# A scan layer in chunks of 64 tokens with two heads stacked, centred weights in front of seven norms, and attention sums first on TensorE

## The chip, the cores and the metric

The kernel runs on one core of a Trainium2 chip. A core has TensorE (PE in the profile, its weight loads PEld), VectorE (DVE), ScalarE (ACT), GpSimd (POOL), a queue that issues most transfers (SP), 128-partition on-chip memory, and eight accumulator banks of 128 x 512 fp32 that TensorE writes. The metric is the device time of one execution in microseconds; lower is better.

## The reference

4096 tokens of width 128 pass through eight residual layers. Each layer is followed by a layer norm without weights, all in fp32:

```python
x = layernorm(x + counter_mix(x))        # layer 0: concat[x, softplus(count)] @ W2
x = layernorm(x + ffn_binarised(x))      # layer 1: gelu(x @ bw1.T + b1) @ bw2.T + b2
x = layernorm(x + channel_attention(x))  # layer 2: per token and head a causal 64 x 64 softmax, then @ Wo + bo
x = layernorm(x + ffn_ternary(x))        # layer 3
x = layernorm(x + gated_linear_attn(x))  # layer 4: o @ Wo
x = layernorm(x + four_experts(x))       # layer 5: relu(x @ W1 + b1) @ W2 + b2, weighted
x = layernorm(x + mamba2(x))             # layer 6: 16 heads of 8 channels, state 64, then @ W_out
x = layernorm(x + kronecker_moe(x))      # layer 7
```

Layer 6 is a linear recurrence over 512 tokens. `dt = softplus(x @ W_dt + b)`, `A = -exp(A_log) * dt`, `B = x @ W_B`, `C = x @ W_C`. With the tokens cut into chunks, a chunk's output is `(C B^T * exp(decay)) X` from inside the chunk (the part `within`) plus `C @ state` from the chunks before (the part `across`), and the state is carried on by `state = state * exp(sum A) + B^T (decayed X)`. The result does not depend on the chunk length; the reference itself uses 64.

## The kernel before

**Tiles and groups.** The tokens are 32 tiles of 128. Eight blocks of four tiles go through layers 0 and 1 (`front`); nine groups (seven of four tiles, two of two, `SIZES`) go through layers 3 to 7.

**Layer 2.** The channel attention is the bulk. Each tile is two units of 64 tokens; each unit is 17 pieces (64 units, 1088 pieces). A piece is a product query x key on DVE (two of 17 on POOL), a subtraction of the row maximum on POOL, an exponential on ACT, a sum over keys on TensorE (`den`), a product with the value on DVE, and a second sum on TensorE (`num`). The pieces live in a ring buffer of `ERING` columns (tile `ringe`); `feed` puts pieces in, `rest` carries each through, `close` finishes a tile and does its norm.

**Order of the work.** No engine order is written by hand. All layers are Python generators that yield the engine they need next. `Order.run` builds one fixed order per engine: it holds an estimated clock for each engine and takes the task that can start first; among tasks within `EPS` = 0.05 us on the same engine the smallest rank wins (`URGE`: close 0, prepare 1, chains 2, rest 3, feed 4). `urge` gives rank 9 to a chain that is ahead of its pace (`LAG`). There are three chains: `chain_a` (fronts and layers 3 to 5), `chain_b` (layer 6), `chain_c` (layer 7). They run beside the attention of later groups; after the last attention piece they are alone. All helpers record their instructions through one line, so nearly every row of the profile says L60, and tiles are told apart by name.

**Matmuls.** `Tensor.matmul` (line 67) splits a product with 128 rows of contraction into column pieces of 32, four of which stand on the array at a time. An fp32 matmul gives two records in the trace.

**A norm** (`norm`, line 545, after layers 0, 1, 3, 4, 5, 6). DVE adds the residual into the accumulator bank, takes `bn_stats` and `bn_aggr` of each tile (`stats`, line 530); ACT makes the reciprocal deviation and the shift (`shifts`) and applies both; TensorE transposes. In layer 5 the residual comes in with the last expert. `close` (line 982) has the same for one tile, with the last step on DVE.

**Layer 6** (line 1309) works on chunks of one tile by four heads: `chunk(j, hq)`, 16 for a group of four tiles. A chunk projects B and C (16 column pieces on TensorE into one bank, one copy by ACT to tile `bc`); ACT multiplies the mask `U` with A for each head (`em`, 128 x 128); TensorE turns that into log decays (`mask16` and `SL` times `em`), ACT takes the exponential. `within` multiplies B and C of each head on TensorE (64 rows, 128 columns, two banks `pg`), DVE multiplies the two halves with `em`, and TensorE adds the product with X (`xp`) to the sums of two tiles. `across` adds `state` x C, transposes B, multiplies it with `dx`, and DVE updates the state with two `scalar_tensor_tensor` (128 x 8 each). `drain` gates the sums; a last matmul with `Wout` and `norm` end the layer.

Of the kernel before, what the change touches and what calls it, by code (L numbers as in the profile page):

```python
# [31 lines left out]
ERING = 8904  # L32
# [6 lines left out]
    "f2_bu": 1, "a3_bdt": 16, "a3_Alog": 16, "f3_sup": 1, "f3_sdn": 1, "bup": 64, "bdn": 32, "rep": 32, "SL": P, "U": P,  # L39
# [98 lines left out]
class Order:  # L138
# [100 lines left out]
    def urge(self, t):  # L239

        if t.rank in self.pace:
            group, steps, size = self.pace[t.rank]
            lag, total = LAG[t.rank]
            if group + size * min(1.0, steps / total) > self.place - (lag if group < HURRY else 0.0):
                return 9
        return self.rank[t.rank]
# [73 lines left out]
class Model:  # L320
# [4 lines left out]
    def __init__(self, ctx, tc, a):  # L325
# [13 lines left out]
            "x": (5, 512), "xT": (5, 512), "a": (6, 512), "b": (12, 512), "c": (4, 512), "gt": (1, 1024), "xp": (2, 152),  # L339
# [76 lines left out]
    def start(self):  # L416
# [23 lines left out]
        for i in range(3):  # L440
            self.d.dma_start(left[32 * i : 32 * i + 2], a["bias"])
        for i in range(3):
            self.v.tensor_copy(part, left[:66])
            self.v.tensor_copy(self.bias[32 * i : 32 * i + 2], part[32 * i : 32 * i + 2])
            self.v.tensor_tensor(left[:66], left[:66], part, ALU.subtract)
# [4 lines left out]
        self.d.dma_start(self.Wo, a["a1_Wo"].rearrange("(c p) d -> p c d", p=P))  # L450

# [7 lines left out]
        self.state = self.keep([P, 8, 32], "state")  # L459
# [3 lines left out]
        self.negA = self.keep([P, H], "negA")  # L463
# [5 lines left out]
        self.mask16 = self.keep([P, P], "mask16", dtype=BF16)  # L469
        self.v.tensor_scalar(self.mask16, self.k["SL"], -30000.0, None, ALU.mult)  # L470
# [73 lines left out]

    def norm(self, g, c, r):

        x = g.x
        mv, rs = yield from self.stats(r, c)
        nm = self.shifts(c, mv, rs)
        for j in range(g.n):  # L550
            self.s.activation(x[:, j, :], r[:, j, :], AF.Identity, scale=rs[:, j : j + 1], bias=nm[:, j : j + 1])
        self.drop(r)
        yield from self.transpose(g.xT, [x[:, j, :] for j in range(g.n)])
# [50 lines left out]
    def count(self, g, nT):  # L604
# [18 lines left out]
        w = yield from self.load("a", self.a["a0_W2"].rearrange("(c p) d -> p c d", p=P), 2, D)  # L623
# [6 lines left out]
        yield "DVE"  # L630
        self.v.tensor_tensor(po, g.x, po, ALU.add)
# [23 lines left out]
    def binarise(self):  # L655

        for half, n, count in ((0, 1, D), (1, 4, 512)):
# [22 lines left out]
            self.v.tensor_tensor(wT, wT, bw, ALU.add)  # L680
            self.drop(ab, bw, alpha)
# [4 lines left out]
            self.drop(wT)  # L686

# [17 lines left out]
    def layer1(self, g):  # L705
# [15 lines left out]
        for j in range(TPG):  # L721
# [3 lines left out]
            for f in range(4):  # L725
                self.pe.matmul(
                    po[:, j, :], lhsT=hT[:, f, j * P : (j + 1) * P], rhs=w2T[:, f * D : (f + 1) * D],
                    start=False, stop=(f == 3),
                )
        yield "DVE"  # L730
        self.v.tensor_tensor(po, g.x, po, ALU.add)
# [250 lines left out]
    def close(self, unit):  # L982
# [22 lines left out]
        if u == 1:  # L1005
# [10 lines left out]
            st, mv, rs = self.small([P, 6], "cst"), self.small([P, 2], "cmv"), self.small([P, 1], "crs")  # L1016
            self.v.tensor_tensor(po, x, po, ALU.add)
            self.v.bn_stats(st, po)
            self.v.bn_aggr(mv, st)
            yield "ACT"  # L1020
            self.rstd(rs, mv[:, 1:2])
            yield "DVE"
            self.v.tensor_scalar(x, po, mv[:, 0:1], rs, ALU.subtract, ALU.mult)
# [10 lines left out]
    def ternarise(self):  # L1034
        self.w3 = []
        for half in range(2):
# [18 lines left out]
            self.v.scalar_tensor_tensor(wT, wT, hi, neg, ALU.is_gt, ALU.subtract)  # L1055
            self.drop(pg, neg)
# [5 lines left out]
    def layer3(self, g):  # L1062
# [37 lines left out]
        for j in range(n):  # L1100
            yield "PE"
            for f in range(4):
                self.pe.matmul(
                    po[:, j, :], lhsT=hT[f][:, j * P : (j + 1) * P], rhs=prT[:, f * D : (f + 1) * D],
                    start=(f == 0), stop=(f == 3),
                )
        yield "DVE"
        self.v.tensor_tensor(po, g.x, po, ALU.add)
# [5 lines left out]
    def layer4(self, g):  # L1114
# [89 lines left out]
        Wo = yield from self.load("a", a["a2_Wo"], D)  # L1204
# [12 lines left out]
        for j in range(n):  # L1217
            self.pe.matmul(po[:, j, :], lhsT=og[:, j * P : (j + 1) * P], rhs=Wo, start=True, stop=True)
        yield "DVE"
        self.v.tensor_tensor(po, g.x, po, ALU.add)  # L1220
# [4 lines left out]
    def layer5(self, g):  # L1225
# [4 lines left out]
        def fetch(e):  # L1230
# [3 lines left out]
            self.d.dma_start(ew[e][1], a["f2_W2"][512 * e : 512 * e + 512].rearrange("(c p) d -> p c d", p=P))  # L1234
# [74 lines left out]
    def layer6(self, g):  # L1309
        a, xT, n = self.a, g.xT, g.n  # L1310
        SL, U = self.k["SL"], self.k["U"]
        yield "SP", self.free("b", 2)
        w, room = self.new("b"), self.new("b")
        X = room[:, : n * D].rearrange("p (j h q) -> p j h q", h=H, q=8)
        wbcs = {}

        def weights():
            for hq in range(4):
                yield "SP", self.free("b", 1 if n == TPG else 6)
                wbcs[hq] = self.new("b")  # L1320
                for i, name in enumerate(("WB", "WC")):
                    self.d.dma_start(wbcs[hq][:, 256 * i : 256 * i + 256], a["a3_" + name][:, 256 * hq : 256 * hq + 256])
# [3 lines left out]
        self.d.dma_start(Wout, a["a3_Wout"])  # L1326
        Xf = X.rearrange("p j h q -> p j (h q)")

        little = room[:, n * D : n * D + 40 * n] if n < TPG else self.small([P, 40 * n], "little", bufs=1)
        dt, A = (little[:, 16 * n * i : 16 * n * (i + 1)].rearrange("p (j h) -> p j h", h=H) for i in range(2))  # L1330
        over = little[:, 32 * n :].rearrange("p (j e) -> p j e", e=8)
# [5 lines left out]
        def inner(j):  # L1337
            yield "PE", self.free("bg")
            ps = self.new("bg")
            self.pe.matmul(ps[:, :144], lhsT=xT[:, j * P : (j + 1) * P], rhs=Wx, start=True, stop=True)  # L1340
            yield "ACT"
            self.s.copy(Xf[:, j, :], ps[:, :D])
            yield "DVE"
            self.v.tensor_tensor(dt[:, j, :], ps[:, D : D + H], self.k["a3_bdt"], ALU.add)
            self.drop(ps)

        yield from self.together(*(inner(j) for j in range(n)))
        yield "ACT", self.free("bg")
        ps = self.new("bg")[:, : 2 * n * H].rearrange("p (i j h) -> p i j h", i=2, h=H)
# [3 lines left out]
        self.v.tensor_tensor(A, dt, self.negA[:, None, :].to_broadcast([P, n, H]), ALU.mult)  # L1353
        yield "DVE"
        self.v.tensor_tensor(X, X, dt[:, :, :, None].to_broadcast([P, n, H, 8]), ALU.mult)
# [4 lines left out]
        pa = ps[:, : 2 * n * H].rearrange("p (i j h) -> p i j h", i=2, h=H)  # L1360
        for i, m in enumerate((SL, self.ones)):
# [5 lines left out]
        for e in range(2):  # L1367
            rows = slice(64 * e, 64 * e + 64)
            self.s.activation(over[rows], pa[rows, 1].rearrange("p j (t e) -> p j t e", e=2)[:, :, :, e], AF.Exp)
        if n == TPG:  # L1370
            dx = self.small([P, n, H, 8], "dx", bufs=1)
            yield "DVE"
        else:
            yield "DVE", self.free("b", 4)
            dx = self.new("b", n, H, 8)
        self.v.tensor_tensor(dx, X, pa[:, 0, :, :, None].to_broadcast([P, n, H, 8]), ALU.mult)
# [18 lines left out]
        def add(t, jj, what, i, lhsT, rhs):  # L1395
            sums, done = bank(t)
            done[i] += 1
            self.pe.matmul(
                sums[32 * i : 32 * i + 32, jj, what, :], lhsT=lhsT, rhs=rhs, start=done[i] == 1, stop=done[i] == 16
            )  # L1400

        def chunk(j, hq):
            cols, at, hs = slice(j * P, (j + 1) * P), 4 * j + hq, slice(4 * hq, 4 * hq + 4)

            yield "PE", self.free(
                "bg", also=lambda: count["begun"] == at and hq in wbcs and min(moved) >= j - 1,
                at=lambda: self.order.until(wbcs[hq]), b=3,
            )
            count["begun"] += 1
            bc, em, ps = self.new("b", 4, P), self.new("b", 4, P), self.new("bg", 4, P)  # L1410
            wbc = wbcs[hq].rearrange("p (i c) -> p i c", c=P)
            for i in range(4):
# [640 lines left out]
```

## Time and profile before

| | us |
|---|---|
| median of three runs (lowest, highest) | 3926.63 (3926.17, 3935.69) |
| the profiled execution, its own time | 3931.12 |
| its span, first to last instruction | 3929.3 |
| busy: PE, PEld | 3079.9, 1610.6 |
| busy: DVE, ACT, POOL | 3258.2, 2605.7, 2920.9 |
| mean granted TensorE clock | 0.909 |

"Busy" of an engine is the time that at least one of its instructions ran. A row of a group view gives count, busy time, mean length in ns, then the idle time of the engine ahead of it and what ended that. A row of the windows view gives the window, its length, and each engine's busy time in it with the number of records. A timeline row gives start, length and the number of instructions merged into it. The trace's first attention product on DVE starts at 88 us, and the last attention sum on TensorE at 3537 us.

### The profile page before, as it was taken

How to read it: one execution, taken by the hardware profiler on the slowest of the kernel's cores; microseconds unless marked ns; L12 is line 12 of the kernel's file. 1: busy time of each engine (PE TensorE's matmuls, PEld its weight loads, DVE VectorE, ACT ScalarE, POOL GpSimd, SP SyncE). 2: the span in 40 equal slices, each digit the busy share in tenths (PEclk: the TensorE clock that was granted, in tenths of full speed). 3: DMA queues.
4: the chain of work that ended last, by engine and by line, in shares of the span. 5: the costliest groups of instructions: out<-in, count | busy, mean ns of one | idle time of the engine just before them, and what ended most of it. 6: DMA issues, size and time to landing. Idle time of an engine off the chain costs nothing.

```text
span 3929.3 us, 128714 instructions
## 1 busy us (share of the span) xinstructions
PE 3079.9 (78%) x55472; PEld 1610.6 (41%) x55472; DVE 3258.2 (83%) x4477; ACT 2605.7 (66%) x4970; POOL 2920.9 (74%) x1320
## 2 busy tenths in 40 slices
PE   6676676777788887977888977888888887879873
PEld 2232222433344443543444543544444443446652
DVE  3779889898998899899898889999989989983421
ACT  5576565667667885677657875787657786666530
POOL 1879997899788887788878877889778987870010
PEclk8798788888899998999999999999989999999986
DMA  3221122212223334243423323343423334424465
GB/s 89 57 53 44 44 59 59 62 44 52 50 59 90 85 79 104 67 117 76 111 61 96 98 74 87 86 126 78 106 64 94 96 88 104 103 63 141 140 154 111
DMA packets 385297, 331.30 MB, mean 84 GB/s; under 512 B 196108, under 2 KB 320460, under 8 KB 384728
## 3 DMA queue, kind: packets, MB, share of 16 engines
q1 hardware_dynamic: 375384, 289.53, 29.8%
q0 software_dynamic: 9344, 33.56, 2.8%
q8 instruction: 434, 7.11, 0.7%
q14 instruction: 135, 1.11, 0.1%
HBM read 147.85 MB, written 40.89 MB: 48 GB/s over the span
## 4 chain that ended last, share of the span: by engine, by line
PE 29%; DVE 27%; ACT 17%; POOL 13%; issue 9%; DMA 4%; SPq 1%; DVEq 0%; POOLq 0%; ACTq 0%
DVE ringe L60 18%; PE bg L60 16%; POOL ringe L60 13%; ACT ringe L60 8%; PE den L60 6%; PE num L60 5%; DVE bg L60 4%; PE kvr L60 3%; ACT ha L60 2%; ACT b L60 1%; ACT L60 1%; ACT bg L60 1%; SPq L60 1%; DVE a L60 1%; DVE b L60 1%
## 5 line engine op out<-in xcount | busy, mean ns | idle before, releaser
L60 POOL TENSOR_TENSOR ringe<-ringe,mr 128x1024 f32<-128x1024 f32 (+13 forms) x1088 | 2557.7, 2386 | 476.1 <-DVE ringe L60 313.3
L60 DVE TENSOR_TENSOR ringe<-ringe,kvr 128x1024 f32<-128x1024 f32 (+14 forms) x1093 | 1287.6, 1208 | 165.3 <-PE den L60 131.5
L60 ACT ACTIVATE ringe<-ringe 128x1664 f32<-128x1664 f32 (+14 forms) x964 | 997.7, 1055 | 600.0 <-POOL ringe L60 597.7
L60 DVE TENSOR_TENSOR ringe<-qr,kvr 128x1024 f32<-128x1024 f32 (+12 forms) x960 | 1103.0, 1184 | 34.7 <-PE num L60 21.1
L60 PE MATMUL den<-ringe,cst 128*32 128x128 f32 (+7 forms) x8744 | 701.8, 416 | 250.5 <-ACT ringe L60 209.4
L60 PE MATMUL num<-ringe,cst 128*32 128x256 f32 (+7 forms) x8720 | 702.5, 410 | 237.6 <-DVE ringe L60 229.8
L60 PEld LDWEIGHTS den<-ringe,cst 128*32 128x32 f32 x8744 | 235.9, 114 | 563.7 <-ACT ringe L60 349.4
L60 PEld LDWEIGHTS num<-ringe,cst 128*32 128x32 f32 x8720 | 227.4, 113 | 566.5 <-DVE ringe L60 440.0
L60 ACT ACTIVATE ringe<-ringe,cst 128x256 f32<-128x256 f32 x512 | 356.7, 780 | 52.1 <-POOL ringe L60 51.9
L60 POOL TENSOR_TENSOR ringe<-qr,ks 128x896 f32<-128x896 f32 (+1 forms) x128 | 287.1, 2243 | 56.0 <-PE num L60 30.0
L60 PE MATMUL bg<-xT,a 128*32 128x512 f32 (+1 forms) x1912 | 253.5, 623 | 34.1 <-DVE a L60 10.0
L60 DVE TENSOR_TENSOR_SCAN bg<-ends,bg 128x512 f32<-128x512 bf16 x128 | 155.0, 1217 | 23.1 <-PE bg L60 22.9
L60 PE MATMUL kvr<-wkv,xT 128*32 128x256 f32 x2048 | 152.0, 419 | 25.9 <-DVE ringe L60 25.6
L60 PE MATMUL bg<-a,ha 128*32 128x128 f32 x4800 | 163.9, 279 | 8.8 <-ACT ha L60 8.5
L60 ACT COPY b<-bg 128x256 f32<-128x256 f32 (+2 forms) x226 | 100.3, 451 | 80.1 <-PE bg L60 75.6
L60 PEld LDWEIGHTS bg<-a,ha 128*32 128x32 f32 x4800 | 132.1, 113 | 30.3 <-issue 14.8
L60 PE MATMUL bg<-xT,b 128*32 128x128 f32 (+1 forms) x3456 | 126.9, 289 | 9.7 <-DVE b L60 3.8
L60 ACT ACTIVATE b<-cst,little 128x128 f32<-128x128 f32 x420 | 133.7, 397 | 0.0
L60 ACT ACTIVATE ha<-bg,cst 128x512 f32<-128x512 f32 (+1 forms) x155 | 100.9, 670 | 38.5 <-PE bg L60 38.1
L60 PE MATMUL bg<-b,cst 128*32 128x512 f32 x856 | 118.9, 627 | 7.9 <-ACT b L60 7.9
L60 PEld LDWEIGHTS bg<-xT,b 128*32 128x32 f32 x3456 | 102.1, 116 | 43.4 <-issue 15.2
L60 PEld LDWEIGHTS bg<-xT,a 128*32 128x32 f32 x1912 | 60.8, 117 | 130.7 <-issue 59.2
(679 smaller groups left out, 4391.5 us busy)
## 6 DMA issues: line engine op xcount, KB each, us to landing
qr<-q SPq DMA_DIRECT2D x512, 128.0 KB
mr<-t SPq DMA_DIRECT2D x512, 128.0 KB
a<-in_f_W SPq DMA_DIRECT2D x67, 256.0 KB
c<-tu SPq DMA_DIRECT2D x204, 64.0 KB
tu<-gt SPq DMA_DIRECT2D x24, 512.0 KB
td<-gt SPq DMA_DIRECT2D x24, 512.0 KB
c<-in_f_Wdn SPq DMA_DIRECT2D x47, 256.0 KB
c<-td SPq DMA_DIRECT2D x88, 128.0 KB
```

Source lines behind the costliest of these rows:

```text
L60: return f(*args, **kw)
```

## The change

Four things change at once.

1. **Layer 6 in chunks of 64 tokens.** The two 64-token halves of a tile (index `c`) are chunks of their own, and an even and an odd head (index `e`) lie on partitions 0 to 63 and 64 to 127 of the same columns. `chunk(j, b)` now covers a tile by eight heads, so there are 8 in place of 16 for a group of four tiles. Its products are 64 x 64 blocks: 16 for `pg` (one bank), 16 for the transposes of B (a matmul with the identity), 16 each of 32 columns for `xp` and `state`, and 16 of 8 columns for `dx`. The decay work (`em`, the mask) is done once for eight heads. The state is carried on twice a tile, each time by two `tensor_tensor` of 128 x 32.
2. **Centred weights.** The mean over the 128 output columns is taken off the last weight and bias ahead of seven norms (layers 0 to 6), by `centre` on DVE. Four of these weights are loaded, centred, stored in device memory and loaded from there when needed (`levelled`). The row mean of `x + layer(x)` is then zero, and the norm needs only the sum of squares: `level` does it all on ACT, with no statistics on DVE.
3. **Residuals.** In layers 1, 3, 4 and 6 TensorE adds the residual (`xT` times the identity), in layer 0 the identity is part of the weight; the DVE addition goes. `close` keeps it.
4. **Order.** On TensorE `rest` (the attention's sums) has the rank of `prepare`, 1, ahead of the chains. `ERING` is 8368 in place of 8904, since `xp`, `state` and the constants are larger.

The diff, cut:

```diff
-ERING = 8904
+ERING = 8368
...
     def urge(self, t):
...
+        if t.rank == "rest" and t.engine == "PE":
+            return self.rank["prepare"]
         return self.rank[t.rank]
...
+    def centre(self, w, n):
+        rows = w.partition_size()
+        w = w.rearrange("p (c d) -> p c d", c=n)
+        s = self.small([P, 8], "mean", bufs=1)[:rows, :n]
+        self.v.tensor_reduce(s, w, AX.X, ALU.add)
+        self.v.tensor_scalar_mul(s, s, 1.0 / D)
+        self.v.tensor_tensor(w, w, s[:, :, None].to_broadcast([rows, n, D]), ALU.subtract)
+
+    def level(self, x, r, rs):
+        n = r.shape[1]
+        for j in range(n):
+            self.s.activation(x[:, j, :], r[:, j, :], AF.Square, accum_out=rs[:, j : j + 1])
+        self.s.activation(rs, rs, AF.Ln, scale=1.0 / D, bias=self.eps)
+        self.s.activation(rs, rs, AF.Exp, scale=-0.5)
+        for j in range(n):
+            self.s.activation(x[:, j, :], r[:, j, :], AF.Copy, scale=rs[:, j : j + 1])
+
     def norm(self, g, c, r):
-        x = g.x
-        mv, rs = yield from self.stats(r, c)
-        nm = self.shifts(c, mv, rs)
-        for j in range(g.n):
-            self.s.activation(x[:, j, :], r[:, j, :], AF.Identity, scale=rs[:, j : j + 1], bias=nm[:, j : j + 1])
+        x, rs = g.x, self.small([P, TPG], c + "rs")[:, : g.n]
+        yield "ACT"
+        self.level(x, r, rs)
...
+    def levelled(self, *names):
+        for name in names:
...
+                w = yield from self.load("a", src[e], n, D)
+                yield "DVE"
...
+                self.centre(w.rearrange("p c d -> p (c d)"), n)
+                yield "SP"
+                put_by = self.keep([P, n * D], name, pool=self.dram)
+                self.d.dma_start(put_by, w.rearrange("p c d -> p (c d)"))
...
     def close(self, unit):
...
             self.v.tensor_tensor(po, x, po, ALU.add)
-            self.v.bn_stats(st, po)
-            self.v.bn_aggr(mv, st)
             yield "ACT"
-            self.rstd(rs, mv[:, 1:2])
-            yield "DVE"
-            self.v.tensor_scalar(x, po, mv[:, 0:1], rs, ALU.subtract, ALU.mult)
+            self.level(x[:, None, :], po[:, None, :], rs)
...
     def layer6(self, g):     (layers 1, 3 and 4 alike at their end)
...
-            self.pe.matmul(po[:, j, :], lhsT=drained[j // 2][:, 0, j % 2, :], rhs=Wout, start=True, stop=True)
-        yield "DVE"
-        self.v.tensor_tensor(po, g.x, po, ALU.add)
+            self.pe.matmul(po[:, j, :], lhsT=drained[j // 2][:, 0, j % 2, :], rhs=Wout, start=True, stop=False)
+            self.pe.matmul(po[:, j, :], lhsT=xT[:, j * P : (j + 1) * P], rhs=self.ident, start=False, stop=True)
...
             def within():
-                    self.pe.matmul(
-                        pg[i % 2][:, i // 2, :], lhsT=bc[rows, i // 2, :], rhs=bc[rows, 2 + i // 2, :], start=True, stop=True
-                    )
...
+                for i in range(4):
+                    for c in range(2):
+                        for e in range(2):
+                            self.pe.matmul(
+                                pg[half(e), i, c], lhsT=part(B, i, c, e), rhs=part(C, i, c, e), start=True, stop=True
+                            )
...
-                for i in range(2):
-                    self.v.tensor_tensor(ev[:, i], ev[:, i], pg[i], ALU.mult)
+                self.v.tensor_tensor(em, em, pg, ALU.mult)
...
             def across():
...
+                def new(c):
+                    s = self.state[:, hs, 24:32]
+                    self.v.tensor_tensor(s, s, over[:, 2 * j + c, hs, None].to_broadcast([P, 4, 8]), ALU.mult)
+                    self.v.tensor_tensor(s, s, got[:, c], ALU.add)
...
+                old(0)
+                yield "ACT"
+                self.s.copy(B, ps.rearrange("p i c s -> p i (c s)"))
...
+                yield "DVE"
+                new(0)
+                yield "PE"
+                old(1)
                 if not last:
...
                     yield "DVE"
+                    new(1)
```

## The prediction

> **What bounds the kernel now.** I read the busy totals first, then the windows view cut where the trace's attention begins (88 us) and ends (3537 us) and where only layer 7 is left (3800 us).
>
> ```profile
> 0.00:88.00 88.00, 58.38 (x736) 26.98 (x736) 25.58 (x67) 47.67 (x119) 6.04 (x14) 0.86 0.26 75
> 88.00:3537.00 3449.00, 2748.50 (x47899) 1383.20 (x47899) 3115.20 (x4025) 2386.95 (x4331) 2889.26 (x1279) 0.92 0.31 79
> 3537.00:3800.00 263.00, 234.52 (x5874) 166.61 (x5869) 101.35 (x330) 154.99 (x462) 14.87 (x16) 0.95 0.55 150
> 3800.00:3930.00 130.00, 38.51 (x977) 33.82 (x971) 16.10 (x58) 16.11 (x58) 10.73 (x12) 0.61 0.48 110
> ```
>
> After the window's length come PE, PEld, DVE, ACT and POOL. In the middle, 3449 us, DVE is busy 90.3%; POOL 84%, PE 80%, ACT 69%. In the tail PE is busy 89% up to 3800, then layer 7's transfers set the pace. So the middle is VectorE's and the tail TensorE's. The waits view over the whole span says how tight that is:
>
> ```profile
> POOL ringe L60 <- DVE ringe L60: 315.3, 106, 22.9
> DVE ringe L60 <- PE den L60: 133.1, 119, 4.6
> DVE state L60 <- PE bg L60: 20.4, 13, 4.7
> ```
>
> POOL's largest wait is for DVE; DVE's largest is for `den`'s sums. The chain that ended last is less one-sided:
>
> ```profile
> PE 29%; DVE 27%; ACT 17%; POOL 13%; issue 9%; DMA 4%; SPq 1%; DVEq 0%; POOLq 0%; ACTq 0%
> ```
>
> **What an instruction costs on DVE** is read from start to start, as neighbours overlap. From DVE's timeline around 2050 to 2071 us:
>
> ```profile
> 2055.62 0.68 DVE L60 TENSOR_TENSOR tb<-bg,epr 128x512 f32<-128x512 f32 x1
> 2056.22 3.87 DVE L60 TENSOR_TENSOR ringe<-qr,kvr 128x1280 f32<-128x1280 f32 x3
> ...
> 2060.27 0.74 DVE L60 TENSOR_TENSOR b<-b,bg 128x256 f32<-128x256 f32 x2
> 2060.93 1.21 DVE L60 TENSOR_TENSOR ringe<-qr,kvr 128x1024 f32<-128x1024 f32 x1
> ...
> 2064.40 0.35 DVE L60 SCALAR_TENSOR_TENSOR state<-state,little,bg 128x8 f32<-128x8 f32 x2
> 2064.67 3.27 DVE L60 TENSOR_TENSOR ringe<-qr,kvr 128x768 f32<-128x768 f32 x6
> ...
> 2070.00 0.27 DVE L60 BATCH_NORM_STATS2 est<-bg 128x6 f32<-128x128 f32 x1
> 2070.30 0.18 DVE L60 BATCH_NORM_AGGREGATE emv<-est 128x2 f32<-128x6 f32 x1
> 2070.40 0.27 DVE L60 BATCH_NORM_STATS2 est<-bg 128x6 f32<-128x128 f32 x1
> ```
>
> A tile's statistics take 0.40 us, a 512-wide product 0.60, two 256-wide ones 0.66, two state updates 0.27.
>
> **DVE, step by step, for the middle alone.** Counts come from the two built instruction orders. Statistics: 193 of the 224 tiles that lose theirs lie in the middle, x 0.40 = -77. Residual additions: some 31 full and 3 half groups there, 31 x 0.60 + 3 x 0.33 = -20. `close`'s last step: its group has a mean of 405 ns, 0.32 net, x 30 = -10. The product with `em`: 198 x 0.33 = 65 become 47 x 0.60 = 28, -37. The state: 174 x 0.135 = 23 become 180 `tensor_tensor` of 128 x 32, a form that the trace lacks; between 0.10 (the update without its wait) and 0.22 (the 0.40 of a statistics pair, which also waits for its own result, less 0.18), I take 0.16, halfway as every second one waits: +6. Centring: seven in the middle, most 512 wide, two passes of 0.60 and a small one: +8. Sum: -130 us of DVE time.
>
> **What becomes of the idle time.** DVE is idle 334 us of the middle. Down: with `rest` first on TensorE the 133 us of waits for `den` may shrink, 0 to -80. Up: the other engines have the same work in less time. PE stays near 80 to 83% by the sum below and POOL goes to 87%; windows of 100 us with PE at 88% have DVE at 97%, so a busy PE need not idle DVE. The smaller ring holds 8.2 mean pieces of 1024 columns in place of 8.7; at worst POOL's waits for DVE grow by that 6%, +19. The state's second step makes DVE wait for PE in the middle of `across`, with attention products queued behind it; at before's rate (20.4 us over 112 steps) it adds little, at a full hop of about 1 us each +60. I take +15, and -60 to +80 as bounds. The middle: -130 + 15 = -115.
>
> **TensorE.** Layer 6's steps stand as runs in PE's timeline, with layer 7 holding runs of just the new shape:
>
> ```profile
> 1538.81 1.15 PE L60 MATMUL bg<-c,hc 64*64 64x64 f32 x32 [2.60 <-ACT last L60]
> ...
> 1544.74 0.71 PE L60 MATMUL bg<-b 64*128 64x128 f32 x8
> 1545.38 0.42 PE L60 MATMUL bg<-b,state 64*32 64x128 f32 x8
> 1545.74 0.44 PE L60 MATMUL bg<-cst,b 128*128 128x128 f32 x2
> ...
> 1547.99 0.29 PE L60 MATMUL bg<-dx,b 128*32 128x8 f32 x16
> 1548.21 0.82 PE L60 MATMUL bg<-c,tb 64*32 64x32 f32 x64
> 1548.96 0.43 PE L60 MATMUL bg<-b,xp 128*32 128x128 f32 x8
> ```
>
> Two old chunks cost, beside their projections (1.06 each, unchanged): decays 2 x 1.44, `pg` 2 x 0.71, `xp` 2 x 0.43, `state` 2 x 0.42, transposes 2 x 2 x 0.22, `dx` 2 x 0.29, 7.5 in all. One new chunk: decay 1.44, `pg`, transposes, `xp`, `state` each 32 records at 1.15, `dx` half of 0.82, 6.5. With 64 chunks -64. The residuals on TensorE: 128 tiles x 8 records, 0.27 (in a run) to 0.40 (alone) us, +35 to +51; smaller projections of X and dt +10. Sum about -10 (-20 to +20): nothing. After its last attention sum the new order leaves 17 of 64 chunks where the old one left 29 of 128, an extra 2.5 units x 6.5 + projections = +20, less the better price of the others (-14), plus residuals +4: +10 in the tail, against norms that no longer cross to DVE there (about 2 us each on the last group's four layers, -9). Tail: 0 (-15 to +25).
>
> The 64*64 run above writes both row halves into one bank, and its 32 records of some 0.24 us stand in 1.15: they overlap. The new `pg` does the same, where the old one had two banks. A rule that speaks against this stands in the Trainium skill, "TensorEngine Tiling (Array Packing)", Restrictions and Gotchas: matmuls of different row tiles cannot use one PSUM bank at the same time. If by it the halves took turns, a block would cost up to twice its 1.15 us; the tail's 68 blocks would add 68 x 1.15 / 0.89 = 88 us, and the time would be 3896. I go by the row.
>
> **ACT, POOL, SP.** ACT loses half of the decay exponentials (64 x 0.59) and the copies' split, and gains squares in place of shifts (0.30 + 0.19 in place of 0.28, but the final scaling drops one operand); between 0 and -45 us, priced at nothing as it is idle for 31% of the middle. POOL's work is the same. SP carries seven loads and seven stores of weights in the first units, with the query copies behind them; a store waits for its centring on DVE. The attention has two units of copies in hand, so 0, at worst +10.
>
> **Start.** Two norms of the first block lie ahead of the first product: in the startup timeline the DVE addition (35.44) to the scaling's end (40.80) takes 5.4 us, on ACT about 3 by the rows above: -4. DVE's four early centrings (6 us) run where it is idle 62 of 88 us.
>
> **Sum.** The profiled execution took 3931.12, 1.8 more than its span of 3929.3. Span after: 3929.3 - 4 - 115 + 0 = 3810; execution 3812. The median of the runs lies 4.5 us below the profiled one: 3808.
>
> **Rivals.**
>
> *DVE's gain is partly off the path.* For it: the chain of waits gives DVE only 27% of the span, 1061 us, a third of its 3258 busy. Then a third of 130 returns, -43 - 4: 3880. Against: 90% busy over 3449 us and POOL waiting for it.
>
> *TensorE becomes the bound, slower.* The small blocks could cost as much per matmul as 128-column ones: 16 matmuls at 0.71 per 4 is 2.84 us a block, 1.69 more. The 68 blocks of the tail (17 chunks x 4), at 89% busy, add 129 us. The middle's 188 blocks raise PE to 2748 + 318 = 3066; at the best share of any 100-us window, 90.6%, that is 3384, only -65. Net +60: 3987. It decides from about 2.65 us a block. Against: the 1.15 us rows. For: the planner gives 64*64 matmuls 0.05 us each, 0.8 a block, so its order is made for less than even the rows show.
>
> *The reordering pays too.* If half of the waits for `den` and part of POOL's go, the middle loses 60 more: 3750.
>
> **Chances.** Forecast 3808 (3770 to 3850): 0.52. Gain partly lost, 3850 to 3915: 0.24. More than forecast, below 3770: 0.08. About no change: 0.05. Slower by TensorE: 0.11. No change means within 0.3%, 12 us, about what a measurement of this kernel can tell. Faster 0.84, same 0.05, slower 0.11. The range for 8 in 10 is 3740 to 3920.
>
> **What would show it.** Right: DVE's busy time falls by about 150 us in all (130 and some 20 outside the middle), its share of the middle stays near 90%, 64*64 runs of `bg<-b` take 1.1 to 1.2 us, the stretch after the last attention sum stays near 392 us. Wrong: DVE's share of the middle falls below 87% (partly lost), or PE's rises above 88% with runs over 2.5 us and a tail over 480 us (TensorE).

## The result

| | median us | lowest, highest | ratio to before, 95% interval |
|---|---|---|---|
| before, 12 runs beside the changed kernel | 3935.43 | 3921.48, 3941.54 | |
| changed, 12 runs | 3941.03 | 3934.68, 3949.19 | 1.0024 [1.0014, 1.0034] |

The changed kernel is slower by a quarter of a per cent, where 3808 us and a range of 3740 to 3920 were forecast. Its profiled execution took 3945.42 us, with a span of 3943.7.

### The profile page after: what moved, and what is told of

Read it like the earlier page. It is cut to its first block, busy times and chain, and to the rows that moved or that the text cites. A ratio compares the mean times of both kernels' runs of the same rounds, so it can differ in the third digit from the quotient of the medians.

```text
span 3943.7 us, 138793 instructions
## 1 busy us (share of the span) xinstructions
PE 3130.9 (79%) x61008; PEld 1764.1 (45%) x61008; DVE 3256.2 (83%) x3812; ACT 2565.5 (65%) x5005; POOL 2921.1 (74%) x1320
## 5 line engine op out<-in xcount | busy, mean ns | idle before, releaser
L60 POOL TENSOR_TENSOR ringe<-ringe,mr 128x1024 f32<-128x1024 f32 (+14 forms) x1088 | 2556.4, 2385 | 484.1 <-DVE ringe L60 332.0
L60 PE MATMUL den<-ringe,cst 128*32 128x256 f32 (+7 forms) x8712 | 704.9, 417 | 235.1 <-ACT ringe L60 206.3
L60 DVE TENSOR_TENSOR state<-state,little 128x32 f32<-128x32 f32 x106 | 153.9, 1452 | 7.4 <-PE kvr L60 5.0
L60 ACT COPY b<-bg 128x512 f32<-128x512 f32 (+1 forms) x178 | 91.4, 528 | 78.1 <-PE bg L60 75.7
L60 POOL DMA_INDIRECT gt<-in_f_tup,dlumps x16 | 15.8, 987 | 153.9 <-ACT dep L60 135.3
L60 ACT ACTIVATE x<-bg 128x128 f32<-128x128 f32 x220 | 57.8, 274 | 79.0 <-PE bg L60 56.8
```

Source lines behind the costliest of these rows:

```text
L60: return f(*args, **kw)
```

## The profile after

The busy totals of the changed kernel:

```profile
PE 3130.9 (79%) x61008; PEld 1764.1 (45%) x61008; DVE 3256.2 (83%) x3812; ACT 2565.5 (65%) x5005; POOL 2921.1 (74%) x1320
```

DVE ran 3812 instructions in place of 4477 and was busy for the same time, 3256.2 us against 3258.2. A fall by about 150 was forecast. The windows view, cut where the first attention product starts (103 us), the attention ends (3555) and only layer 7 is left (3815):

```profile
0.00:103.00 103.00, 61.92 (x771) 31.01 (x771) 25.73 (x53) 50.22 (x137) 4.44 (x13) 0.82 0.23 67
103.00:3555.00 3452.00, 2779.49 (x52079) 1500.76 (x52083) 3125.94 (x3438) 2352.70 (x4350) 2894.84 (x1283) 0.92 0.32 81
3555.00:3815.00 260.00, 244.15 (x6729) 192.61 (x6721) 83.83 (x255) 144.17 (x452) 11.10 (x12) 0.97 0.47 125
3815.00:3944.00 129.00, 45.33 (x1438) 39.73 (x1438) 20.65 (x67) 18.45 (x67) 10.71 (x12) 0.66 0.51 120
```

The third number after the window's length is DVE's busy time. The middle is as long as before (3452 against 3449), DVE's share of it is still 90.6%, the tail is 389 against 392, and the start is 15 us longer. So nothing was hidden or moved off the path. DVE simply did not get faster. Its groups, with shapes kept apart, say where the time is (count, busy us, mean ns, idle ahead):

```profile
L60 DVE TENSOR_TENSOR state<-state,little 128x32 f32<-128x32 f32 x106 | 153.9, 1452 | 7.4 <-PE kvr L60 5.0 <-PE bg L60 2.4
L60 DVE TENSOR_TENSOR state<-state,bg 128x32 f32<-128x32 f32 x111 | 20.8, 187 | 31.1 <-PE bg L60 21.3 <-ACT b L60 2.7
```

These are the two instructions of the new state update, of one shape. The add takes 187 ns. The multiply takes 1452 ns in the mean, and its fastest 157. They differ in where their inputs lie: the add reads `state` from on-chip memory (SBUF) and `got` from an accumulator bank (PSUM); the multiply reads `state` and `over`, both in SBUF. DVE's timeline and POOL's for the same moment (start, length):

```profile
838.02 2.15 DVE L60 TENSOR_TENSOR ringe<-ringe,kvr 128x1920 f32<-128x1920 f32 x1
840.08 1.52 DVE L60 TENSOR_TENSOR state<-state,little 128x32 f32<-128x32 f32 x1
841.63 0.19 DVE L60 TENSOR_TENSOR state<-state,bg 128x32 f32<-128x32 f32 x1
841.74 1.62 DVE L60 TENSOR_TENSOR ringe<-qr,kvr 128x1408 f32<-128x1408 f32 x1
```

```profile
837.78 3.77 POOL L60 TENSOR_TENSOR ringe<-ringe,mr 128x1664 f32<-128x1664 f32 x1
841.51 2.77 POOL L60 TENSOR_TENSOR ringe<-qr,ks 128x1536 f32<-128x1536 f32 x1
```

POOL's instruction ends at 837.78 + 3.77 = 841.55. The multiply, started at 840.08, ends at 841.60, within 0.05 of it. The attention products before and after it read `kvr`, which lies in PSUM, and run beside POOL undisturbed. Of the 106 multiplies in this group 71 started with POOL busy: they took 2077 ns in the mean, and 70 of them ended within 0.15 us of the end of a POOL instruction (of the 56 adds that started beside a busy POOL, one did). The 35 that found POOL idle took 183 ns. So 71 x 1.9 = 134 us of DVE's "busy" time is waiting. No view of waits shows it, since no semaphore is involved.

The rule is in the Trainium skill, "SBUF — State Buffer", Who interferes with whom: a DVE instruction with two SBUF inputs and a GpSimd instruction that reads SBUF exclude each other through a shared read port; the one that comes second is blocked for the whole of the other. The rows of DVE agree, 2077 ns against 183; whether such a multiply ever holds POOL in turn is not shown here.

## The experiments

Theory **port**: the loss is the multiply held by POOL. First rival, **absorbed**: it only takes up time in which DVE would have waited anyway. Second rival, **order**: the new rank on TensorE starves the chains. "Middle" below runs from the first attention product on DVE to the last normalisation (`rd`), "tail" from there to the end. The median of before was 3929 to 3935 us beside the different runs; differences between kernels are therefore taken from the ratios, times 3932.

**e1**, an operand in PSUM:

```diff
-                    self.v.tensor_tensor(s, s, over[:, 2 * j + c, hs, None].to_broadcast([P, 4, 8]), ALU.mult)
+                    self.v.tensor_tensor(s, s, decayed[:, c], ALU.mult)
                     self.v.tensor_tensor(s, s, got[:, c], ALU.add)
...
                 self.s.copy(B, ps.rearrange("p i c s -> p i (c s)"))
+                decayed = ps.rearrange("p i c s -> p (i c s)")[:, 64:128].rearrange("p (c i q) -> p c i q", c=2, q=8)
+                self.s.copy(decayed, over[:, 2 * j : 2 * j + 2, hs, None].to_broadcast([P, 2, 4, 8]))
```

> The changed kernel with one difference: ACT copies the two decay factors of a step into 64 free columns of the step's PSUM bank, so that the state's multiply (128x32) has one operand in PSUM. Theory 'port': a DVE instruction with both inputs in SBUF waits for the end of the POOL instruction that is running (in the changed kernel 71 of the 106 multiplies found POOL busy and took 2077 ns in the mean, 70 of them ended with POOL's instruction; the 35 others took 183 ns). Then all multiplies take about 190 ns, DVE's busy time falls by about 134 us to about 3120, and the run is 3805 to 3840 us, near the 3812 forecast for the change. Rival 'absorbed': the multiply only takes up time in which DVE would have waited anyway for layer 6's longer chain or for TensorE; then DVE's busy time falls by as much, its idle time grows by as much, and the run stays within 0.5% of the changed kernel's 3941.

Measured: 3861.46 us, ratio 0.9837 [0.9823, 0.9851]. Multiplies and adds now stand in one group:

```profile
L60 DVE TENSOR_TENSOR state<-state,bg 128x32 f32<-128x32 f32 x210 | 38.3, 183 | 30.6 <-PE bg L60 21.3 <-ACT ha L60 3.6 <-PE kvr L60 1.9
```

DVE's busy time fell by 130 to 3126.6. The port theory had the rows right and the gain too large: 74 us came, not 100 to 135. In the middle 126 us of DVE's busy time went (3127 to 3000), but its idle time grew by 35 (326 to 361), and the tail by 10. So a part of the hold had taken the place of waits.

**e2**, the fused form of the kernel before, head by head:

```diff
-                    self.v.tensor_tensor(s, s, over[:, 2 * j + c, hs, None].to_broadcast([P, 4, 8]), ALU.mult)
-                    self.v.tensor_tensor(s, s, got[:, c], ALU.add)
+                    for i in range(4):
+                        s, h = self.state[:, 4 * b + i, 24:32], 4 * b + i
+                        self.v.scalar_tensor_tensor(s, s, over[:, 2 * j + c, h : h + 1], got[:, c, i], ALU.mult, ALU.add)
```

> The changed kernel with the state updated head by head, multiply and add in one instruction as in the kernel before (scalar_tensor_tensor, 128x8, the decay as a scalar of each partition, the addend in PSUM): about 480 instructions in place of about 240. Theory 'port': none of them is held by POOL, because one of the two tensor inputs lies in PSUM (the kernel before had 222 of them at 214 ns); DVE's busy time is 154 + 24 less and 480 x 0.21 = 103 more, some 75 us less than in the changed kernel; the run is 3850 to 3890. Rival 'absorbed': within 0.5% of the changed kernel's.

Measured: 3854.92, ratio 0.9819 [0.9803, 0.9834], 81 us less than the changed kernel, in the expected range. The updates take 214 ns as in the kernel before, and the 330 that started beside a busy POOL no longer than the 150 others (214 and 216 ns). So the decay, a scalar of each partition that lies in SBUF, does not act as a second SBUF tensor here:

```profile
L60 DVE SCALAR_TENSOR_TENSOR state<-state,little,bg 128x8 f32<-128x8 f32 x400 | 61.4, 214 | 5.7 <-PE bg L60 3.7 <-PE kvr L60 1.9
```

These updates overlap one another (400 of 214 ns are busy for 61.4 us), so DVE's busy time fell by 101 where some 75 was expected.

**e3**, the same fault planted in the kernel before:

```diff
-                    for pr in range(2):
-                        s = self.state[:, 2 * hq + pr, 8 * hq : 8 * hq + 8]
-                        self.v.scalar_tensor_tensor(
-                            s, s, over[:, j, 2 * hq + pr : 2 * hq + pr + 1], ps[:, 2 + pr, :8], ALU.mult, ALU.add
-                        )
+                    s, both = self.state[:, 2 * hq : 2 * hq + 2, 8 * hq : 8 * hq + 8], slice(2 * hq, 2 * hq + 2)
+                    self.v.tensor_tensor(s, s, over[:, j, both, None].to_broadcast([P, 2, 8]), ALU.mult)
+                    self.v.tensor_tensor(s, s, ps[:, 2:4, :8], ALU.add)
```

> The kernel before with one difference: its state update, two fused instructions a step, becomes a multiply with both inputs in SBUF (128x16) and an add with one in PSUM, about 111 of each. Theory 'port': two thirds of the multiplies find POOL busy and last until its instruction ends (mean 1.2 to 1.5 us), DVE's busy time grows by 110 to 150 us in a stretch where it is the bound, and the run is 4030 to 4070. Rival 'absorbed': DVE's rows are no longer than 0.2 us, or its idle time shrinks by what they grow, and the run stays within 0.5% of the kernel before.

Measured: 4056.46, ratio 1.0337 [1.0316, 1.0358], +132 us.

```profile
L60 DVE TENSOR_TENSOR state<-state,little 128x16 f32<-128x16 f32 x100 | 121.6, 1216 | 0.0
```

All 74 multiplies that found POOL busy ended with a POOL instruction (1585 ns), the 26 others took 166. DVE's busy time in the middle rose by 105, a little under the 110 to 150 expected. "Absorbed" falls with e1, e2 and e3 as an account of the whole; of e1's 126 us it describes the 35 above.

**e4**, the changed kernel without the two lines in `urge` that put the sums first.

> The changed kernel without the new order on TensorE (the attention's sums no longer go first); all else as changed. The forecast put this part at 0 to -80 us (value about 0 beside the rest). Theory 'port': the loss of the changed kernel is in the state's multiply, so this kernel too is near the changed one or slower, 3941 to 4000, with the multiply's mean still above 1 us. Rival 'order': the new order starves the chains that feed the attention (the first attention product came 15 us later than before); then this kernel is faster than the changed one by 40 us or more.

Measured: 4079.19, ratio 1.0374 [1.0354, 1.0394], outside what either theory said. "Order" falls as a cause of the loss. But the new order is worth 138 us here, where the forecast took about nothing.

**The parts apart.** So I ran the cube of the three parts, with the fused state update throughout: f1 to f4, then its last corners h1 and h2. The diffs are parts of the one shown. The ring goes with layer 6: f1, f3 and h1 have 8904 columns, f4 and h2 8176, f2 and e2 8368. What it is worth by itself is not told apart from layer 6 here (h3 below has it alone).

> The kernel before with only the new order on TensorE (the attention's sums go first). Theory 'own gain': the order is worth about as much here as in the changed kernel, where leaving it out cost 138 us (3941 to 4079): the run is 3800 to 3860, with DVE's idle time in the middle down by 60 to 100 us and its busy time unchanged. Theory 'repair': the order only makes good a wait that the new layer 6 brings (its two dependent state steps, its many small matmuls); then the run is within 0.5% of the kernel before, 3910 to 3950.

> The changed kernel with the fused state update (as in e2, 3855) but without the new order on TensorE. Both theories expect it slower than 3855; by 'own gain' and by 'repair' alike 80 to 140 us, thus 3935 to 3995, which would make centred norms and new layer 6 together no gain without the order. If it is below 3890 instead, the order's worth in the changed kernel came from the slow multiply, and a third account is needed: a DVE held by POOL profits most from sums that come early.

> The kernel before with the centred norms and the new order, layer 6 as before (chunks of 128, fused state update). By the forecast's terms DVE loses 77 + 20 + 10 us and gains some 22 by the centring (its rows in e1), -85, and the start is 13 later: 3855 if the order is worth nothing here. 'Own gain' takes another 60 to 100 off: 3755 to 3795. 'Repair': 3840 to 3870.

> The kernel before with the new layer 6 (fused state update, 480 instructions of 0.21 us) and the new order, norms as before (ring 8176, 192 less than in the changed kernel, for the statistics' tiles). DVE: products -37, state +55, so +18 us. 'Own gain': 3929 + 18 less what the order is worth beyond the new layer 6's own wait, 3850 to 3940. 'Repair': 3930 to 3980.

> The kernel before with only the centred norms. DVE loses 77 + 20 + 10 us and gains some 22 by the centring. Theory 'DVE-bound': without the order the middle shrinks by most of these 85 us and the start grows by 13; with a tail as before the run is 3845 to 3890. Theory 'sums late': on TensorE the attention's sums come behind the chains' matmuls as before, so DVE gets idle instead of faster; idle time in the middle grows by 40 us or more and the run is 3890 to 3940.

> The kernel before with only the new layer 6 (fused state update; ring 8176). DVE's work is 18 us more. 'DVE-bound': 3935 to 3965. 'Sums late': the new layer's twice as many 64-row matmuls stand ahead of the attention's sums, DVE's idle time in the middle grows by 60 to 110 us as in e4 and f2 (424 and 423 against 334), and the run is 3985 to 4050; then the order, which costs 51 us without this layer, gains 30 to 90 with it (f4: 3959).

The eight corners and the changed kernel, with the profiled execution's stretches in us (idle is DVE's, in the middle):

| kernel | run | ratio, 95% interval | start | middle | DVE busy | idle | tail |
|---|---|---|---|---|---|---|---|
| before | 3929 to 3935 | | 88 | 3450 | 3116 | 334 | 391 |
| order alone (f1) | 3982 | 1.0130 [1.0114, 1.0145] | 90 | 3363 | 3073 | 290 | 525 |
| norms alone (h1) | 3926 | 0.9989 [0.9980, 0.9999] | 102 | 3431 | 3040 | 391 | 394 |
| layer 6 alone (h2) | 4019 | 1.0218 [1.0202, 1.0233] | 91 | 3504 | 3106 | 398 | 424 |
| norms, order (f3) | 3940 | 1.0027 [1.0018, 1.0037] | 102 | 3302 | 2991 | 311 | 535 |
| layer 6, order (f4) | 3959 | 1.0071 [1.0053, 1.0088] | 89 | 3487 | 3117 | 371 | 381 |
| norms, layer 6 (f2) | 3969 | 1.0087 [1.0070, 1.0105] | 101 | 3447 | 3024 | 423 | 426 |
| all three (e2) | 3855 | 0.9819 [0.9803, 0.9834] | 101 | 3376 | 3021 | 354 | 376 |
| changed | 3941 | 1.0024 [1.0014, 1.0034] | 103 | 3453 | 3127 | 326 | 388 |

f2 and f4 fall in a stated range, "repair" for f4; f1 and f3 lie outside of both theories'. No column of times adds up by parts. DVE's busy time comes nearest: the norms take 76 us off (h1). But alone they bring 4 us of run time, because DVE's idle time grows by 58; its waits for `den`, over the whole span, go from 133.1 to 195.7 us:

```profile
DVE ringe L60 <- PE den L60: 195.7, 148, 5.4
```

This is h1's line of the waits view. Run and idle time are in the range of "sums late", and h2's too (idle +64). But the account behind it, sums that wait behind the chains' matmuls, holds for one kind of sum only. With the sums put first, DVE's waits for `num` (those at `ringe` and `rd` together) fall from 56 to 32 us between h1 and f3, 102 to 50 between h2 and f4, and 90 to 47 between f2 and e2. Those for `den` stay or grow: 196 and 192, 159 and 174, and for f2 and e2

```profile
DVE ringe L60 <- PE den L60: 183.0, 164, 5.5
DVE ringe L60 <- PE den L60: 192.5, 186, 4.9
```

Why the norms lengthen the waits for `den` is therefore not shown. The order alone shortens the middle by 87. Half of that is DVE's idle time (-44); the other half is DVE work (-43) that moves, with the chains' matmuls that gave way, to the tail, which grows by 134. f1's windows:

```profile
90.00:3453.00 3363.00, 2664.01 (x45761) 1311.84 (x45765) 3072.60 (x3891) 2345.71 (x4153) 2886.22 (x1274) 0.92 0.31 77
3453.00:3978.00 525.00, 373.66 (x8983) 270.28 (x8975) 161.29 (x520) 230.14 (x698) 29.42 (x32) 0.83 0.48 124
```

PE has 374 us of work in its tail, 273 in that of before. With the new layer 6 the tail stays at 376 to 388 under the same order; e2's windows:

```profile
101.00:3477.00 3376.00, 2775.12 (x52471) 1494.51 (x52471) 3021.33 (x3635) 2370.47 (x4400) 2891.88 (x1279) 0.92 0.32 82
3477.00:3853.00 376.00, 272.82 (x7775) 224.12 (x7771) 108.11 (x365) 145.73 (x470) 25.60 (x28) 0.85 0.52 135
```

The new layer 6 by itself costs 86 us (h2). Only with it does the order pay: 105 us between f2 and e2, 58 between h2 and f4; without it the order costs 51 (f1) and 15 (h1 to f3). Neither "own gain" nor "repair" covers this. It is an exchange between middle and tail that turns out differently with each layer 6.

**g1 to g3**: is that exchange the pace count? Chain B's count in `LAG` becomes 234 in e2 (g1), 360 in f1 (g2) and in f3 (g3):

```diff
-LAG = {"chain_a": (0.7, 300), "chain_b": (1.6, 290), "chain_c": (2.6, 132)}
+LAG = {"chain_a": (0.7, 300), "chain_b": (1.6, 360), "chain_c": (2.6, 132)}
```

> As e2 (the changed kernel with the fused state update, 3855), but chain B's step count in LAG goes from 290 to 234. The scheduler holds a chain back once its group number plus its steps over this count is ahead of the attention. Layer 6 before took 310 to 323 steps a group in chain B, the new one takes 253 to 256, and the count stayed 290; 234 gives the new layer the old ratio. Theory 'pace': a good part of what the new layer 6 does for the tail (376 us in e2 against 534 in f3, both with norms and order) is only this, so the middle gets shorter by 20 to 60 us, the tail longer by 60 to 140, the run 3885 to 3950. Rival 'layer': the tail is short because the new layer 6 is itself shorter; the run stays at 3840 to 3875.

> As f1 (the kernel before with only the new order, 3982: middle 3363, tail 525), but chain B's step count 360 instead of 290, so that the old layer 6's 310 to 323 steps count as the new one's 255 do against 290. 'Pace': chain B keeps its turn longer, the tail falls by 60 to 140 us, the middle grows by 20 to 60, the run is 3870 to 3930. 'Layer': within 0.5% of f1, 3962 to 4000.

> As f3 (norms and order with the old layer 6, 3940: middle 3302, tail 534), with chain B's step count 360. 'Pace': tail 400 to 470, middle 3320 to 3360, run 3830 to 3895. 'Layer': within 0.5% of f3, 3920 to 3960.

Measured: 3863.43, 3957.30 and 3903.88 us; tails 394, 490 and 474 in place of 376, 525 and 535; middles 3368, 3369 and 3327 in place of 3376, 3363 and 3302. Every tail and every middle moves the way "pace" says, but nearly all by less than it says (g3's middle alone is in its range): g1's run is in the range of "layer", g2's and g3's lie between the two. The count is at most a part of it.

**g4**: the first norm as before (`norm0` is the old `norm`).

```diff
...
-        w = yield from self.load("a", self.level_w["a0_W2"][0], 2, D)
+        w = yield from self.load("a", self.a["a0_W2"].rearrange("(c p) d -> p c d", p=P), 2, D)
...
+        yield "DVE"
+        self.v.tensor_tensor(po, g.x, po, ALU.add)
         self.drop(z, w)
-        yield from self.norm(g, "a%d" % (g.k % 2), po)
+        yield from self.norm0(g, "de"[g.k % 2], po)
...
-            self.order.spawn(self.levelled("a0_W2"), "chain_a")
```

> As e2, but the norm behind a0_W2 is done as in the kernel before (statistics and residual on DVE, weight loaded straight from its input, not centred, stored and loaded again). In the changed kernel and in e2 the first attention product is 13 to 15 us later than before. If the weight's way through DRAM is the cause, the first product is 8 to 14 us earlier than in e2, and DVE's busy time in the middle is about 15 to 20 us more (8 groups of one add and four statistics); the run is within 10 us of e2. If the cause is the centring of the other weights in the start, the first product stays where it is and the run is 10 to 25 us longer than e2.

Measured: 3873.39, ratio 0.9850 [0.9835, 0.9865]. The first attention product is 9.5 us earlier than in e2 (91.8 and 101.3), so most of the late start is the weight's way through device memory. DVE's busy time grows by 11 us, and the run by 12, a little over the 10 allowed.

**h3** (before with `ERING = 8368`) and **h4** (e2 with the centring on ACT):

```diff
-        self.v.tensor_scalar_mul(s, s, 1.0 / D)
-        self.v.tensor_tensor(w, w, s[:, :, None].to_broadcast([rows, n, D]), ALU.subtract)
+        self.s.activation(s, s, AF.Copy, scale=-1.0 / D)
+        for c in range(n):
+            self.s.activation(w[:, c, :], w[:, c, :], AF.Identity, bias=s[:, c : c + 1])
```

> The kernel before with only the smaller ring, 8368 elements instead of 8904. The forecast gave this at most +19 us. If the ring bounds how far the attention's stages run ahead, the middle is 10 to 20 us longer; if not, the run is within 0.3% of the kernel before. A difference of either sign within 10 us is also what any edit does that reshuffles the schedule.

> As e2 (3855), but the centring of weights subtracts the mean on ACT, piece by piece, and ACT also scales the mean. In the changed kernel the 128x512 subtractions on DVE took 1904 ns in the mean (690 with POOL idle, 3117 with POOL busy) and the 128x4 scalings 753 ns. Theory 'port': these DVE rows vanish, DVE's busy time falls by 20 to 25 us, the run is 3830 to 3855. Rival 'covered': they lie beside other waits, and the run is within 0.3% of e2.

Measured: h3 3955.24, ratio 1.0061 [1.0046, 1.0077], the middle 34 longer (more than either bound) and the tail 10 shorter. h4 3853.86, ratio 0.9800 [0.9786, 0.9814]: 18 us of DVE time gone from the middle, 16 of them back as idle time (354 to 370). The run lies in both stated ranges and differs from e2's by 7 us (by the ratios), less than the intervals, so it does not decide. The idle time speaks for "covered".

**i1, i2**: how much is the shuffle? `EPS = 0.06` in place of 0.05, in before and in e2.

> The kernel before with the scheduler's tie window 0.06 us instead of 0.05: the same instructions, some in another order. If a shuffle alone is worth little, the run is within 0.3% of the kernel before, and the smaller ring's 23 us are the ring's; if it moves the run by 15 us or more either way, differences of that size between kernels here have no cause that can be named.

> e2 (3855) with the tie window 0.06 us: the same instructions, some in another order. Little: 3843 to 3867. Shuffle matters: outside of that by up to 30 us, and then the pace's 8 us (g1), the first norm's 18 (g4) and the centring on ACT (h4) can't be told from it.

Measured: i1 3929.28, ratio 0.9995 [0.9985, 1.0005], but with a middle 22 longer and a tail 26 shorter. i2 3900.30, ratio 0.9918 [0.9904, 0.9931]: the same work as e2 in another order is 39 us slower, more than the 30 expected at most, with DVE busy for 3024 us of the middle (e2: 3021) and idle for 396 (354). By i1 alone, which stayed within its 0.3%, h3's 24 us would be the ring's; i2 shows that an order alone can do as much.

This limits what the rest shows. The run times of g1 to g4, h3 and h4 differ from their neighbours' by no more than that and are no evidence of a cause; f1's 51 us are hardly more. Beyond it stand the planted fault (+132), its two cures (-74 and -81), and the order within norms and layer 6 (-105, and -138 with the slow multiply) and with layer 6 alone (-58), and the new layer 6 alone (+86). The changed kernel itself was not shuffled. Repaired versions, e1, e2, g1, g4, h4 and the shuffled one, lie between 3854 and 3900, all faster than both kernels; e2 and h4 are the fastest and can't be told apart.

## Why the prediction was wrong

**The step that failed** is the state's term: "180 `tensor_tensor` of 128 x 32, a form that the trace lacks; between 0.10 [...] and 0.22 [...]: +6". In the middle the rows of the state's update sum to 167.8 us in place of 37.3 (forecast: 29 in place of 23), because the multiply, with both inputs in SBUF, is held by POOL. Taking the hold away (e1) takes 126 us off DVE's busy time there. The bounds came from rows of like size, not of like operands. Rows of like operands were in the group view of before (by shape), two of each; the first has two tensors in SBUF, the second goes from SBUF to SBUF with one:

```profile
L60 DVE SCALAR_TENSOR_TENSOR a<-a,ter_hi,a 128x512 f32<-128x512 f32 x2 | 2.8, 1408 | 0.1
L60 DVE TENSOR_SCALAR a<-a,ter_lo 128x512 f32<-128x512 f32 x2 | 2.4, 1220 | 0.0
```

Their means hide 752 and 2065 ns in the first, 478 and 1961 in the second, with POOL idle and busy. From them a bound of "to the end of POOL's instruction" could have been had. As an estimate: POOL is busy 84% of the middle at 2.3 us an instruction, so about 90 multiplies x 0.84 x half of that, 1.13, are 85 us. That would have put the forecast near 3890, nearer to no change, though still short: a held multiply lost 1.9 us in the mean, not 1.13 (some sat through more than one POOL instruction).

**With that one term mended** the sum reads 3808 + 126 = 3934, and 3941 was measured. That is partly luck. In e1, where the multiply is no longer held and the other terms stand alone, the profiled execution took 3861 in place of 3812: the start is 17 us worse than forecast, the middle 26 and the tail 7. In the changed kernel the held multiplies hid some of that. Term by term:

- *Statistics, additions, `close`, `em`* (-77, -20, -10, -37). Confirmed. In the middle their rows went from 124.0, 32.1, 12.6 and 96.3 us to 35.1, 8.9, 0 and 47.3; rows overlap, so busy time falls by less. e1's busy time is 116 below that of before, against a forecast of 130. Of the 14 between them the next point is 16, and the state's rows (33.6 us in e1) give 10 back.
- *Centring* (+8). 24.2 us: the same hold. Three 128 x 512 subtractions with POOL busy took 3117 ns in the mean, three with POOL idle 691. Both groups of rows, these and the small scalings between them:

```profile
L60 DVE TENSOR_TENSOR a<-a,mean 128x512 f32<-128x512 f32 x6 | 11.4, 1904 | 0.2
L60 DVE TENSOR_SCALAR mean<-mean 128x4 f32<-128x4 f32 x6 | 4.5, 753 | 0.2
```

- *Idle time* (+15, bounds -60 to +80). -8 in the changed kernel, whose held multiplies swallow waits; +27 in e1, +21 in e2, +62 in i2, so the bounds were right and the point value had no basis: it depends on the schedule. Two of its parts were misread. "`rest` first" was to shrink the waits for `den`; in the four pairs of the cube it changed them by -4 to +15, and only from e4 to the changed kernel, where the multiply is held, do they fall clearly (187 to 154). What it shortens are waits for `num` and others: e2's idle time is 69 below that of f2. "The state's second step", up to +60, is small: DVE's waits for PE at `state`, over the whole span, go from 25 us in before to 31 in e2 and 47 in f2 and in the changed kernel. f2's idle time, without the order, is 89 above that of before; h1 and h2 put 58 and 64 of such time to the norms alone and to layer 6 alone, which the forecast did not have.
- *Start* (-4). +15. I counted the centrings as hidden by DVE's idle time and did not follow `a0_W2`: its reload is issued at 40.03 us, behind the loads of `wkv` in SP's queue, and TensorE's first product with it waited 5.95 us for it, on the way of the first block.
- *Tail* (0). -3. That the tail depends on how far the order lets the chains fall behind (376 to 535 us in the cube) was not in the forecast at all.
- *TensorE*. Confirmed in the price of a block, not in the sum: PE's busy time rose by 51 us (3079.9 to 3130.9; 29 in e2), where -20 to +20 was forecast. Most of that is `dx`: its 32 records a chunk, of 8 columns, take 1.10 us, nearly as long as 64 columns, where 0.41 was priced, and 64 chunks x 0.69 are 44 us. The new runs of 64*64 blocks take 1.15 us, as layer 7's had. From PE's timeline of the changed kernel:

```profile
1510.82 1.15 PE L60 MATMUL bg<-b,b 64*64 64x64 f32 x32
1811.20 1.10 PE L60 MATMUL bg<-dx,b 64*64 64x8 f32 x32
```

  The rule on row tiles in one bank that the prediction set aside (the Trainium skill, "TensorEngine Tiling (Array Packing)", Restrictions and Gotchas) did not bring the doubled price that was worked out from it. No run here has the same products in two banks beside it.

The rivals: TensorE as the bound is ruled out by those 1.15 us and by the tail. "Partly off the path" had the right effect for the norms alone (76 us of DVE work, 4 us of time) and for a part of e1's gain (126 and 74); it was not what made the changed kernel slow, where DVE's share of the middle stayed above 90%.

**Open**: why the new layer 6 keeps the tail short under the order. The pace count moves the tail by 18, 35 and 61 us (g1, g2, g3) of up to 159, where the shuffle moved it by 26 (i1). And how much of the 74 to 81 us that the cures bring is the hold and how much a lucky order; the shuffled e2 is still 42 below the changed kernel.

## What to carry to other kernels

Before pricing a DVE instruction, note where each of its inputs lies and what POOL does at that time: with two tensor inputs in SBUF beside a busy POOL its price here was the rest of POOL's instruction, whatever its size, now and then of the next ones too, and the profile books that as busy time. Group rows by tile and shape and compare the fastest with the mean; here a factor of nine between them was a wait without a semaphore. Where a scheduler sets the order, run one kernel that changes nothing but the order before explaining small differences: here that alone was 39 us in one kernel and 2 in another.

## What the runs showed of the hardware

- Size does not decide the hold. Beside the instructions with two SBUF tensors, `TENSOR_SCALAR` from SBUF to SBUF on 128 x 4 took 1044 ns in the mean with POOL busy and 170 with POOL idle, and all four held ones ended with POOL's instruction; on 128 x 1 it took 154 ns beside a busy POOL. On 128 x 4 from PSUM (`wn<-bg`) 21 of them beside a busy POOL took 160 to 163 ns. `TENSOR_REDUCE` of 128 x 512 took 673 ns beside a busy POOL and 682 beside an idle one. A `SCALAR_TENSOR_TENSOR` with two SBUF tensors was held as well (2729 against 751 ns in the changed kernel).
- A held instruction can sit through more than one POOL instruction: the longest multiply took 8198 ns, to the end of the third POOL instruction after the one that ran when it started, and one of 6448 started before the end of one POOL instruction and ended with the next.
